# A four-layer graph network on one core: late transpositions of x, the last layer's scale and shift, and the order of the units behind the last score

## The chip, the cores and the metric

The kernel runs on one core of one Trainium2 chip. The metric is the device time of one execution in microseconds (us). The kernel before takes 3922.26 us, the median of three runs (3920.86 to 3927.18).

## What is computed

The input is x, 16 batches of 1024 nodes with 128 features, and one adjacency matrix of 1024 x 1024 that all batches share (about 1 in 64 entries set). Three attention layers follow each other, each with weights of its own, and then a fourth, last layer of another kind:

```python
# layers 0, 1, 2 (8 heads of 16)
Q, K, V = h @ Wq, h @ Wk, h @ Wv
scores = einsum('bnhd,bmhd->bhnm', Q, K) / 4
attn = softmax(where(adj == 0, -inf, scores))
x = layer_norm(h + (attn @ V) @ Wo + bo, ln1_g, ln1_b)
x = layer_norm(x + relu(x @ W1 + b1) @ W2 + b2, ln2_g, ln2_b)
# last layer
h = x @ W
e = leaky_relu((h @ a_src)[:, :, None] + (h @ a_dst)[:, None, :])   # slope 0.2
att = softmax(where(adj == 0, -inf, e))
out = ln_gamma * normalised(att @ h + x) + ln_beta
```

## The kernel before, in words

**Blocks and turns.** The work is cut into 48 blocks, each one attention layer of one batch. Four batches (LANES) form a group: layer 0 of the four, then layer 1 of the four, then layer 2 of the four, then the next group (L835). A block has 32 turns: two head groups g, two halves of the queries qh, eight tiles of keys kt. One turn of the main loop (L958 to L995) does a score step, an attention step four turns behind it (AHEAD), and one piece of the other work.

- The score step (L535) makes four matmuls of Q against K (L545), two for each of two PSUM slots "s". In most turns the first slot goes through ACT's exponential (L553) and is then multiplied by the mask on POOL (L554); the second gets the mask added on DVE (L557) and its exponential on ACT after that (L569). In the ten turns of BOTH_ON_DVE both go the second way, so POOL has no mask to do.
- The attention step (L574) multiplies the tile e by V and the row of ones, and accumulates in one bank. After eight steps, finish (L577) transposes the sums on DVE, takes reciprocals and multiplies on POOL (L589).

**Other work: chains of tasks.** Everything else stands in chains. A task is (gap, function, tiles, and for some a mark); put (L842) adds them, take (L852) runs one, is_due (L867) says when: `gap` turns after the task before it in the chain, or at the turn that a table AT gives for the chains "xP", "proj" and "post". piece (L871) runs once a turn: it takes every due task whose tiles text has a "*" (it uses no TensorE), but only one task without a star. That one task is called a unit below. "+w", "-x" and the like count work tiles taken and given back (TILES): x has five, one more than the lanes. need (L880) forces a chain on until a mark is done. All units share one PSUM bank "t"; edge units use the "s" slots.

**Who orders what.** PE, ACT and SP (the DMA queue that issues all loads and stores) run in the order in which the program is written, turn by turn. DVE and POOL are ordered by a scheduler, and issue_after pins some of their instructions behind the score step's.

**The x of the next group.** A batch's x is loaded (fetch, a unit of SP) when one of the five x tiles is free, that is, when a batch of the group before has stored its result. Where x is there by turn 22 two blocks ahead, its transposed copy is made through DRAM. Otherwise (late x) transpose_x (L496) with by_dma=False puts the two transpositions on TensorE (L345 in transpose_half) into the chain "xP", at turns 4 and 6 of the block ahead of its own. transpose_x also puts POOL's `scale` (multiplication by the gain of the layer before, L511, none for layer 0) and `shift` (addition of bo, L515), 6 or 2 turns on. Six projection units follow from turn 9 (AT_V_LAST), and stack (L523) lays Q and K out by DMAs on SP.

**The last layer** (last_tasks, L701) is a chain behind the last attention layer of each batch, so it runs in the blocks that follow it:

- xt(0), xt(1): two transpositions; nodes: three units of x @ W (L730 to L737) with POOL's multiplication of x by the gain (L798 in by_rows) taken behind the second and the addition of the bias behind the third;
- rows_gh (L742): one transposition of the per-node exponentials; send_rows (L749): eight DMAs on SP into the rows g_rows and h_rows (L756, L757);
- edges(v) (L761): eight matmuls from these rows (L769) and four DVE operations with the mask (L774) into an edge tile, of which there are two;
- aggregate(v) (L779): 32 matmuls (by_columns, L383), then DVE adds x (L785) and takes statistics. After v = 3 and v = 7, normalise scales four tiles on POOL (L433 to L435, L441);
- gain and bias of each half by POOL (by_rows, L798) and the stores on SP (L812), which give back the x tile.

Edge unit v+1 and aggregate v are one task, two turns from the one before.

**The end.** In the last block the halves of the queries are ordered so that the first half of its attention is complete earlier. Its post work runs as two short chains "final" (the list `alone`, L687: gather, output projection, x1t three turns later, two units of W1, one of W2), and the last layer of batch 15 behind them. After the last score turn (n = 1536) eight more main-loop turns take one unit each. Then the tail loop (L1002) counts turns on, and takes in each turn one due task of every chain.

Of the kernel before, what the change touches and what calls it, by code (L numbers as in the profile page):

```python
# [29 lines left out]
LANES = 4  # L30
FIRST = 1


AT = {"xP": (4, 6), "proj": (5, 7, 9, 11, 17, 19), "post": (13, 15, 17, 18, 21, 22, 22, 23, 24, 25, 27, 29, 31, 35, 38, 40)}
AT_V_LAST = (9, 11, 17, 19, 20, 21)
AT_FIRST = (12, 14, 16, 18, 20, 22)
T_AT = 22
STACK_AT = 24
AT_END = {3: (12, 21, 22, 24, 25, 26, 27, 28, 30, 31), 2: (8, 9, 13, 14, 15, 16, 17, 18, 20, 21)}
AHEAD = 4  # L40
BOTH_ON_DVE = (3, 7, 8, 15, 23, 24, 26, 28, 30, 31)
TILES = {"w": 8, "x": LANES + 1, "last": 2}
BLOCKED = -57344.0
# [76 lines left out]
def fast_path(ctx: ExitStack, tc: tile.TileContext, a: dict, out: bass.AP, flag):  # L120
# [375 lines left out]
    def transpose_x(m, by_dma=True):  # L496
        b, l = blocks[m]
        x, xT = state["x", b], xt_tile("xT")
        state["xT", m] = xT
        if by_dma:  # L500
            put(moved(lambda: xT, lambda: x), ("xT", m))
        elif m == 0:
            for h in range(2):
                transpose_half(xT[:, h], x, h)
        else:
            put([(0, lambda: transpose_half(xT[:, 0], x, 0), ""), (0, lambda: transpose_half(xT[:, 1], x, 1), "")],
                ("xP", m), first=True)

        def scale():
            with tc.issue_after(behind["pool"]) if m else nullcontext():  # L510
                nc.gpsimd.tensor_mul(x, x, rows(W[l - 1]["ln2_g"]))  # L511

        def shift():
            with tc.issue_after(behind["pool"]) if m else nullcontext():
                nc.gpsimd.tensor_add(x, x, rows(W[l]["bo"]))  # L515
        if m:
            put(([(6, scale, "*")] if l else []) + [(2 if l else 6, shift, "*")], ("shifted", m))
        else:
            shift()

# [73 lines left out]
    def post_tasks(m, quick=False):  # L594
        b, l = blocks[m]
        w = W[l]
        s = {}
        att, recs = state["A"], state["recs"]

        def gather(h):  # L600
            def run():
                s["aT", h] = half_tile("aT")
                nc.vector.transpose(s["aT", h], att[:, h].rearrange("p k g d -> p (k g d)"))
                if h == 1:
                    check_range(recs.rearrange("p g h k -> p (g h k)"))
            return run

        def out_proj(h):
            def run():
                if h == 0:  # L610
                    need_if(("shifted", m))
                    s["n1"] = with_stats(state["x", b])
                project([s["aT", h]], [w["Wo"]], h, add_and_stats(s["n1"]))
                normalise(s["n1"], slice(4 * h, 4 * h + 4))
            return run

        def x1t(h, alone=False):
            def run():
                x1 = s["n1"][0]
                if h == 0:  # L620
                    s["x1T"] = xt_tile("x1T")
                transpose_half(s["x1T"][:, h], x1, h)
                if alone:
                    scale_shift(x1[:, 4 * h:4 * h + 4, :], w["ln1_g"], w["b2"])
                elif h == 1:
                    scale_shift(x1, w["ln1_g"], w["b2"])
            return run

        def x1_by(op, v):
            def run():  # L630
                with tc.issue_after(behind["pool"]):
                    op(s["n1"][0], s["n1"][0], rows(w[v]))  # L632
            return run

        def normed(ts):
            def run():
                with tc.issue_after(behind["pool"]):
                    if ts.start == 0:
                        scalars(s["n2"], slice(0, NT))
                    subtract_scale(s["n2"], ts)  # L640
            return run

        def ffn1(f, h):
            def run():
                s["h", f, h] = half_tile("hT")
                ps = bank()
                by_columns(ps, w["W1"][:, f * P:(f + 1) * P], s["x1T"][:, h])
                with soon():
                    nc.scalar.activation(s["h", f, h], ps, AF.Relu, bias=w["b1"][:, f:f + 1], scale=1.0)  # L649
            return run  # L650

        def ffn2(h, alone=False):
            def run():
                if h == 0:
                    s["n2"] = with_stats(state["x", b])
                project([s["h", f, h] for f in range(NF)], [w["W2"][:, f, :] for f in range(NF)], h,
                        add_and_stats(s["n2"]))
                if alone:
                    normalise(s["n2"], slice(4 * h, 4 * h + 4))
            return run  # L660

        def both():
            with tc.issue_after(behind["dve"]):
                gather(0)()
                gather(1)()


        def x1():
            return s["n1"][0]

        def x1T():
            if "x1T" not in s:
                s["x1T"] = xt_tile("x1T")
            return s["x1T"]

        together = [(6, both, "+w +w *"), (1, out_proj(0), "-w"), (1, out_proj(1), "-w")]
        if quick:
            together += [(5, x1t(0), ""), (1, x1t(1), "")]
            together += [(1, ffn1(f, h), "+w") for h in range(2) for f in range(2)]
            together += [(1, ffn2(0, True), "-w -w"), (1, ffn2(1, True), "-w -w")]  # L680
        else:
            together += moved(x1T, x1)
            together += [(0, x1_by(nc.gpsimd.tensor_mul, "ln1_g"), "*"), (1, ffn1(0, 0), "+w"),
                         (0, x1_by(nc.gpsimd.tensor_add, "b2"), "*"), (1, ffn1(1, 0), "+w"), (2, ffn1(0, 1), "+w"),
                         (1, ffn1(1, 1), "+w"), (1, ffn2(0), "-w -w"), (1, ffn2(1), "-w -w"),
                         (3, normed(slice(0, 4)), "*"), (2, normed(slice(4, NT)), "*")]
        alone = [[(1, gather(h), "+w"), (1, out_proj(h), "-w"), (3, x1t(h, True), ""), (1, ffn1(0, h), "+w"),  # L687
                  (1, ffn1(1, h), "+w"), (1, ffn2(h, True), "-w -w")] for h in range(2)]
        return together, alone

# [10 lines left out]
    def last_tasks(b):  # L701
# [3 lines left out]
        def xt(h):  # L705
            def run():
                w = W[L - 1]
                if h == 0:

                    s["col"] = work.tile([P, 4, NT], F32, tag="col", name="col", bufs=2)  # L710
                    s["hd"] = [work.tile([P, 4, D + 1], F32, tag="w", name="hd", bufs=TILES["w"]) for _ in range(2)]
                    s["n"] = with_stats(state["x", b])
                s["xT", h] = half_tile("xT")
                transpose_half(s["xT", h], state["x", b], h, w["ln2_gc"], w["ln2_bc"])
            return run

        def nodes(t0, t1):
# [43 lines left out]
        def edges(v):  # L761
# [14 lines left out]
                                                   1.0, mask01[:, :, q:q + SLOT], op0=OP.max, op1=OP.mult)  # L776
            return run

        def aggregate(v):  # L779
            def run():  # L780
                e, ps = s["e", v], bank()
                for t in range(NT):
                    by_columns(ps[:, :D + 1], e[:, t, :], s["hd"][t // 4][:, t % 4, :], start=(t == 0), stop=(t == NT - 1))
# [1 line left out]
                nc.vector.scalar_tensor_tensor(s["n"][0][:, v, :], ps[:, :D], s["col"][:, 3, v:v + 1],  # L785
                                               state["x", b][:, v, :], op0=OP.mult, op1=OP.add)
                stats(s["n"], slice(v, v + 1))
                if v % 4 == 3:
                    with tc.issue_after(behind["pool"]):
                        normalise(s["n"], slice(v - 3, v + 1))  # L790
                if v == NT - 1:
                    check_range(s["col"].rearrange("p c t -> p (c t)"))
            return run
# [22 lines left out]
        def two(f, g):  # L816
            def run():
# [1 line left out]
                g()  # L819
            return run  # L820

        mul, add = nc.gpsimd.tensor_mul, nc.gpsimd.tensor_add
        tasks = [(5, xt(0), "+w +last +w +w"), (1, xt(1), "+w"), (2, nodes(0, 3), ""), (2, nodes(3, 6), ""),
                 (0, by_rows(mul, x, lambda: W[L - 1]["ln2_g"]), "*"), (2, nodes(6, 8), "-w -w"),
                 (0, by_rows(add, x, lambda: ln2_b_last), "*"), (2, rows_gh, ""), (1, send_rows, "*"), (7, edges(0), "")]
        for v in range(NT - 1):
            tasks.append((2, two(edges(v + 1), aggregate(v)), ""))
            if v in (4, 6):
                tasks.append((0, by_rows((mul, add)[v // 2 - 2], y(0), lambda v=v: wl[("ln_gamma", "ln_beta")[v // 2 - 2]], 4), "*"))
        tasks += [(2, aggregate(NT - 1), ""), (2, store(0), "-last -w -w *"), (1, by_rows(mul, y(1), lambda: wl["ln_gamma"], 4), "*"),  # L830
                  (2, by_rows(add, y(1), lambda: wl["ln_beta"], 4), "*"), (3, store(1), "-x *")]
        return tasks


# [17 lines left out]
    def take(chain):  # L852
# [3 lines left out]
            return False  # L856
        chain["queue"].popleft()
        f()
        for t in tiles.replace("*", "").split():
            free[t[1:]] += -1 if t[0] == "+" else 1  # L860
        done.add(mark)
        chain["due"] = now[0]
# [2 lines left out]
        return True  # L865

    def is_due(chain):  # L867
        gap, at = chain["queue"][0][0], chain["queue"][0][4]
        return now[0] >= max(chain["due"] + gap, at or 0)

    def piece():  # L871
# [371 lines left out]
```

## Time and profile before

| What | Value |
|---|---|
| runs, median (lowest to highest) | 3922.26 us (3920.86 to 3927.18) |
| the profiled execution, own time | 3922.55 us |
| its span | 3920.7 us |
| mean granted TensorE clock | 0.983 |
| PE busy | 3715.7 us |
| POOL busy | 3477.6 us |
| DVE busy | 3460.5 us |
| ACT busy | 3296.9 us |
| L554 (POOL's mask), one | 2029 ns, 1056 times |
| L574 (attention), one of the 12288 matmuls | 602 ns modelled, 1629.0 us busy in all |
| last score turn starts | 3800.1 us |

The trace gives every instruction its start, duration, and the idle time of its engine ahead of it in square brackets, with what ended it. "t" is the bank of the units, "acc" that of the attention step, "s" the slots of the scores. Times in the trace count from the start of the span, which is 1.85 us shorter than the execution's own time. Blocks and turns are not named in the trace; turn k of block m begins with the (32 m + k)th group of four L545 matmuls.

An ordinary block takes about 70.4 us. The blocks with last-layer work are longer: blocks 10 to 15 take 76.5, 94.2, 90.5, 92.4, 98.2 and 83.7 us, and those of the two groups after it are alike.

### The profile page before, as it was taken

Reading aid. Unit: us, or ns where it says so; the run is one execution under the profiler, and the core shown is the slowest. Engines: PE = TensorE matmul, PEld = TensorE weight load, DVE = VectorE, ACT = ScalarE, POOL = GpSimd, SP = SyncE. Lnnn points to the kernel's source line nnn. Section 1 sums busy time; section 2 is a strip of 40 time slices with the busy share of each in tenths; the row PEclk is TensorE's granted clock in tenths of the full one; section 3 lists DMA queues with packets and bytes.
Section 4 is the critical chain, followed back from the end, with each engine's and each line's share of the span. In section 5 each row is a group of like instructions: output and inputs, shape, how many; then the busy total and the mean of one; then the engine's idle time right before and its main releaser. Section 6 shows DMA issues by size and latency. Waiting matters only on the chain.

```text
span 3920.7 us, 109674 instructions
## 1 busy us (share of the span) xinstructions
PE 3715.7 (95%) x44385; PEld 1515.1 (39%) x44385; DVE 3460.5 (88%) x5860; ACT 3296.9 (84%) x3797; POOL 3477.6 (89%) x2971
## 2 busy tenths in 40 slices
PE   7999999999989999999998999999999999999987
PEld 2333333344434333334443333333444433333346
DVE  6999999989878999998897899998898889999876
ACT  7989999977877999997777899999777789999850
POOL 5899999988978999998878899999887899999885
PEclk8999999999999999999999999999999999999998
DMA  5424334322323334332222324334232323424200
GB/s 139 113 73 103 91 81 110 76 70 70 89 63 79 98 72 110 80 95 73 72 67 76 92 66 101 95 74 100 73 82 52 88 71 93 103 71 106 63 8 21
DMA packets 245887, 319.28 MB, mean 81 GB/s; under 512 B 51072, under 2 KB 174208, under 8 KB 245376
## 3 DMA queue, kind: packets, MB, share of 16 engines
q1 hardware_dynamic: 243840, 311.52, 31.7%
q8 instruction: 353, 5.78, 0.6%
q14 instruction: 158, 1.29, 0.1%
q10 hardware_dynamic: 1536, 0.68, 0.1%
HBM read 58.53 MB, written 51.38 MB: 28 GB/s over the span
## 4 chain that ended last, share of the span: by engine, by line
POOL 46%; PE 38%; ACT 5%; DVE 5%; issue 3%; SPq 2%; DMA 1%; DVEq 0%; ACTq 0%; POOLq 0%
POOL e L554 27%; PE acc L574 13%; PE t L383 12%; PE s L545 9%; POOL x L441 7%; POOL mv L435 4%; POOL x L632 4%; ACT e L553 3%; DVE e L557 3%; ACT e L569 2%; PE s L769 2%; POOL x L798 2%; PE s L383 1%; POOL A L589 1%; SPq L530 1%
## 5 line engine op out<-in xcount | busy, mean ns | idle before, releaser
L557 DVE TENSOR_TENSOR e<-s,mask_add 128x1024 f32<-128x1024 f32 x2016 | 2377.4, 1211 | 240.3 <-PE s L545 214.5
L554 POOL TENSOR_TENSOR e<-e,mask 128x1024 f32<-128x1024 f32 x1056 | 2120.1, 2029 | 241.6 <-ACT e L553 227.8
L569 ACT ACTIVATE e<-e 128x1024 f32<-128x1024 f32 x2016 | 2110.9, 1062 | 185.2 <-DVE e L557 156.3
L574 PE MATMUL acc<-e,v 128*17 128x512 f32 x12288 | 1629.0, 602 | 78.6 <-POOL e L554 64.8
L553 ACT ACTIVATE e<-s 128x1024 f32<-128x1024 f32 x1056 | 1083.3, 1026 | 250.6 <-PE s L545 244.8
L545 PE MATMUL s<-Wq,Wk 64*128 64x512 f32 x6144 | 1196.4, 458 | 32.3 <-DVE e L557 21.1
L545 PEld LDWEIGHTS s<-Wq,Wk 64*128 64x128 f32 x6144 | 499.8, 185 | 1085.2 <-issue 388.9
L574 PEld LDWEIGHTS acc<-e,v 128*17 128x17 f32 x12288 | 205.2, 96 | 595.2 <-issue 351.1
L441 POOL TENSOR_SCALAR x<-x,mv 128x128 f32<-128x128 f32 x896 | 388.1, 448 | 19.1
L435 POOL TENSOR_TENSOR mv<-mv,half_neg 128x4 f32<-128x4 f32 (+1 forms) x179 | 214.0, 1195 | 13.6
L413 DVE BATCH_NORM_STATS2 st<-x 128x6 f32<-128x128 f32 x896 | 204.0, 281 | 7.7
L383 PE MATMUL t<-hd,ee 128*32 128x129 f32 x6656 | 205.7, 275 | 2.5 <-DVE x L420 2.4
L383 PE MATMUL t<-x1T,W 128*32 128x512 f32 x1520 | 201.9, 603 | 0.3
L774 DVE SCALAR_TENSOR_TENSOR ee<-s,mask 128x256 f32<-128x256 f32 x512 | 179.8, 413 | 23.4 <-PE s L769 23.4
L383 PEld LDWEIGHTS t<-W,hT 128*32 128x32 f32 x6080 | 170.9, 111 | 59.5 <-issue 48.4
L383 PEld LDWEIGHTS t<-hd,ee 128*32 128x32 f32 x6656 | 178.8, 110 | 16.1 <-DVE x L420 5.8
L383 PE MATMUL t<-W,hT 128*32 128x128 f32 x6080 | 184.7, 274 | 0.1
L589 POOL TENSOR_TENSOR A<-tt,recs 128x256 f32<-128x256 f32 x192 | 119.8, 624 | 49.7 <-DVE recs L588 49.6
L420 DVE TENSOR_TENSOR x<-t,x 128x512 f32<-128x512 f32 x191 | 129.1, 676 | 38.3 <-PE t L383 38.0
L649 ACT ACTIVATE hT<-t,b 128x512 f32<-128x512 f32 x190 | 130.4, 686 | 23.3 <-PE t L383 22.5
L585 DVE STREAM_TRANSPOSE tt<-acc 128x512 f32<-128x512 f32 x192 | 135.3, 705 | 0.0
L357 DVE STREAM_TRANSPOSE xb<-x 128x512 f32<-128x512 f32 x164 | 115.0, 701 | 20.1 <-POOL x L441 19.9
(145 smaller groups left out, 2531.1 us busy)
## 6 DMA issues: line engine op xcount, KB each, us to landing
Wk<-hi SPq DMA_DIRECT2D x384, 128.0 KB
Wk<-lo SPq DMA_DIRECT2D x384, 128.0 KB
Wq<-hi SPq DMA_DIRECT2D x384, 128.0 KB
Wq<-lo SPq DMA_DIRECT2D x384, 128.0 KB
tr<-xb SPq DMA_DIRECT2D x656, 64.0 KB
x1T<-tr SPq DMA_DIRECT2D x90, 256.0 KB
xT<-tr SPq DMA_DIRECT2D x74, 256.0 KB
x<-in_x_dram SPq DMA_DIRECT2D x124, 64.0 KB
```

The source lines that it names most:

```text
L383: nc.tensor.matmul(dst[j:j + SLOT, :], cols, rhs, start=start, stop=stop)
L413: nc.vector.bn_stats(st[:, t, :], z[:, t, :])
L435: nc.gpsimd.tensor_tensor(v, v, half_neg[:, ts], OP.pow)
L441: nc.gpsimd.tensor_scalar(z[:, t, :], z[:, t, :], mv[:, t, 0:1], mv[:, t, 1:2], op0=OP.add, op1=OP.mult)
L545: nc.tensor.matmul(ps[:, r * 512:(r + 1) * 512], k[64 * r:64 * r + 64, kt * P:(kt + 1) * P], q[64 * r:64 * r + 64, q0:q0 + 512], start=Tru ...
L553: nc.scalar.activation(ev, psv, AF.Exp, scale=HD ** -0.5)
L554: behind["pool"] = nc.gpsimd.tensor_mul(ev, ev, m).ins
L557: behind["dve"] = nc.vector.tensor_add(ev, psv, m).ins
L569: nc.scalar.activation(ev, ev, AF.Exp, scale=HD ** -0.5)
L574: nc.tensor.matmul(acc[j * SLOT:j * SLOT + HD + 1, :], v_bufs[m % 2][:, kt, 2 * j + g, :], e[:, j, :], start=first, stop=last)
L589: nc.gpsimd.tensor_mul(state["A"][:, qh, :, g, :], tt[:, :, :HD], rec[:, :, None].to_broadcast([P, 16, HD]))
L774: nc.vector.scalar_tensor_tensor(e[:, :, j * SLOT:(j + 1) * SLOT], ps.rearrange("p (k q) -> p k q", q=P)[:, :, j * SLOT:(j + 1) * SLOT], 1 ...
```

## The change

It touches the planner alone; no operation is added, removed or resized.

- **Late x.** The two transpositions of a late x are due at turns 7 and 8 of the block, not 4 and 6. POOL's shift of a late x is due 31 turns after it is put, not 6.
- **Scale and shift of the last layer.** The multiplication and the addition of x leave the list of last-layer tasks. They become a chain of their own, "scaled", which xt(1) puts. A mark "~" in their tiles text lets them run only in turns 0 to 6, 22 and 23 of a block (POOL_FREE) as long as the tail has not begun. aggregate forces them if they have not run yet.
- **The fourth batch of a group** (not the very last batch): the normalisation of its second half is no longer part of aggregate(7) but a task after store(0). That task and the gain and bias of this half have the mark "^": turns 30, 31 and 0 to 6 only.
- **Behind the last score turn** (n of 1536 or more) a gap of 2 counts as 1, so a chain of last-layer units can take one unit every turn. The last batch's first edge unit follows its rows after 4 turns, not 7.
- **The end.** In the chain of the second half of the very last attention, x1t comes five turns after the output projection, not three.

```diff
-AT = {"xP": (4, 6), ...
+AT = {"xP": (7, 8), ...
+POOL_FREE = {"~": (0, 1, 2, 3, 4, 5, 6, 22, 23), "^": (30, 31, 0, 1, 2, 3, 4, 5, 6)}
...
-            put(([(6, scale, "*")] if l else []) + [(2 if l else 6, shift, "*")], ("shifted", m))
+            put(([(6, scale, "*")] if l else []) + [(2 if l else 6 if by_dma else 31, shift, "*")], ("shifted", m))
...
-        alone = [[(1, gather(h), "+w"), (1, out_proj(h), "-w"), (3, x1t(h, True), ""), ...
+        alone = [[(1, gather(h), "+w"), (1, out_proj(h), "-w"), (3 + 2 * h, x1t(h, True), ""), ...
...
                 transpose_half(s["xT", h], state["x", b], h, w["ln2_gc"], w["ln2_bc"])
+                if h == 1:
+                    put([(1, by_rows(mul, x, lambda: W[L - 1]["ln2_g"]), "*~"),
+                         (2, by_rows(add, x, lambda: ln2_b_last), "*~")], ("scaled", b), first=True)
...
+        late = b % LANES == LANES - 1 and b < B - 1
+
+        def norm(h):
+            def run():
+                with tc.issue_after(behind["pool"]):
+                    normalise(s["n"], slice(4 * h, 4 * h + 4))
+            return run
...
         def aggregate(v):
             def run():
+                need_if(("scaled", b))
...
-                if v % 4 == 3:
-                    with tc.issue_after(behind["pool"]):
-                        normalise(s["n"], slice(v - 3, v + 1))
+                if v % 4 == 3 and (v < NT - 1 or not late):
+                    norm(v // 4)()
...
-                 (0, by_rows(mul, x, lambda: W[L - 1]["ln2_g"]), "*"), (2, nodes(6, 8), "-w -w"),
-                 (0, by_rows(add, x, lambda: ln2_b_last), "*"), (2, rows_gh, ""), (1, send_rows, "*"), (7, edges(0), "")]
+                 (2, nodes(6, 8), "-w -w"), (2, rows_gh, ""), (1, send_rows, "*"), (7 if b < B - 1 else 4, edges(0), "")]
...
+        up = "*^" if late else "*"
+        tasks += [(2, aggregate(NT - 1), ""), (2, store(0), "-last -w -w *")] + [(0, norm(1), up)] * late
+        tasks += [(1, by_rows(mul, y(1), lambda: wl["ln_gamma"], 4), up), (2 - late, by_rows(add, y(1), lambda: wl["ln_beta"], 4), up),
+                  (3, store(1), "-x *")]
...
     def is_due(chain):
-        gap, at = chain["queue"][0][0], chain["queue"][0][4]
+        gap, tiles, at = chain["queue"][0][0], chain["queue"][0][2], chain["queue"][0][4]
+        if now[0] >= 4 * NT * len(blocks):
+            gap -= gap == 2
+        for c in POOL_FREE:
+            if c in tiles and not tail[0] and now[0] % (4 * NT) not in POOL_FREE[c]:
+                return False
         return now[0] >= max(chain["due"] + gap, at or 0)
```

More of the change, by code (lines that the diff above doesn't have):

```diff
@@ L31 @@
 FIRST = 1
-AT = {"xP": (4, 6), "proj": (5, 7, 9, 11, 17, 19), "post": (13, 15, 17, 18, 21, 22, 22, 23, 24, 25, 27, 29, 31, 35, 38, 40)}
+AT = {"xP": (7, 8), "proj": (5, 7, 9, 11, 17, 19), "post": (13, 15, 17, 18, 21, 22, 22, 23, 24, 25, 27, 29, 31, 35, 38, 40)}
 AT_V_LAST = (9, 11, 17, 19, 20, 21)
@@ L686, in post_tasks @@
                          (3, normed(slice(0, 4)), "*"), (2, normed(slice(4, NT)), "*")]
-        alone = [[(1, gather(h), "+w"), (1, out_proj(h), "-w"), (3, x1t(h, True), ""), (1, ffn1(0, h), "+w"),
+        alone = [[(1, gather(h), "+w"), (1, out_proj(h), "-w"), (3 + 2 * h, x1t(h, True), ""), (1, ffn1(0, h), "+w"),
                   (1, ffn1(1, h), "+w"), (1, ffn2(h, True), "-w -w")] for h in range(2)]
@@ L777, in edges @@
             return run
+        mul, add = nc.gpsimd.tensor_mul, nc.gpsimd.tensor_add
+        late = b % LANES == LANES - 1 and b < B - 1
[4 more added lines that the diff above has]
+            return run
         def aggregate(v):
             def run():
+                need_if(("scaled", b))
                 e, ps = s["e", v], bank()
@@ L820, in two @@
             return run
-        mul, add = nc.gpsimd.tensor_mul, nc.gpsimd.tensor_add
         tasks = [(5, xt(0), "+w +last +w +w"), (1, xt(1), "+w"), (2, nodes(0, 3), ""), (2, nodes(3, 6), ""),
-                 (0, by_rows(mul, x, lambda: W[L - 1]["ln2_g"]), "*"), (2, nodes(6, 8), "-w -w"),
-                 (0, by_rows(add, x, lambda: ln2_b_last), "*"), (2, rows_gh, ""), (1, send_rows, "*"), (7, edges(0), "")]
+                 (2, nodes(6, 8), "-w -w"), (2, rows_gh, ""), (1, send_rows, "*"), (7 if b < B - 1 else 4, edges(0), "")]
         for v in range(NT - 1):
@@ L829, in last_tasks @@
                 tasks.append((0, by_rows((mul, add)[v // 2 - 2], y(0), lambda v=v: wl[("ln_gamma", "ln_beta")[v // 2 - 2]], 4), "*"))
-        tasks += [(2, aggregate(NT - 1), ""), (2, store(0), "-last -w -w *"), (1, by_rows(mul, y(1), lambda: wl["ln_gamma"], 4), "*"),
-                  (2, by_rows(add, y(1), lambda: wl["ln_beta"], 4), "*"), (3, store(1), "-x *")]
+        up = "*^" if late else "*"
+        tasks += [(2, aggregate(NT - 1), ""), (2, store(0), "-last -w -w *")] + [(0, norm(1), up)] * late
+        tasks += [(1, by_rows(mul, y(1), lambda: wl["ln_gamma"], 4), up), (2 - late, by_rows(add, y(1), lambda: wl["ln_beta"], 4), up),
+                  (3, store(1), "-x *")]
         return tasks
@@ L858, in take @@
         f()
-        for t in tiles.replace("*", "").split():
+        for t in tiles.translate(str.maketrans("", "", "*~^")).split():
             free[t[1:]] += -1 if t[0] == "+" else 1
```

## The prediction

> **What bounds the kernel now.** I read the page first: TensorE (PE) is busy 95% of the span, so only the 5% it misses can be won.
>
> ```profile
> span 3920.7 us, 109674 instructions
> PE 3715.7 (95%) x44385; PEld 1515.1 (39%) x44385; DVE 3460.5 (88%) x5860; ACT 3296.9 (84%) x3797; POOL 3477.6 (89%) x2971
> PEclk8999999999999999999999999999999999999998
> ```
>
> Then the waits, longest first. Two of PE's own matter: for a DMA of x (three times, up to 7.8 us), and for POOL's masking of e (130 times).
>
> ```profile
> PE acc L574 <- POOL e L554: 64.8, 130, 2.5
> PE t L345 <- DMA x<-in_x_dram: 21.0, 3, 7.8
> ```
>
> Then the timelines of PE, SP and POOL around one such wait, in block 14 turn 4 (the four score matmuls of L545 mark a turn; blocks are counted from 0, 32 turns each). PE stands 7.80 us and starts again at half clock (1.22 us for a score step, otherwise 0.73).
>
> ```profile
> 1108.73 1.05 PE L574 MATMUL acc<-e,v 128*17 128x512 f32 x8
> 1117.58 1.08 PE L345 MATMUL t<-identf,x 128*128 128x128 f32 x4 [7.80 <-DMA x<-in_x_dram]
> 1118.59 1.22 PE L545 MATMUL s<-Wq,Wk 64*128 64x512 f32 x4
> ```
>
> ```profile
> 1090.31 20.66 SPq L812 DMA_DIRECT2D out_dram<-x  x8
> 1112.47 3.66 SPq L167 DMA_DIRECT2D x<-in_x_dram  x8
> ```
>
> ```profile
> 1099.87 2.02 POOL L554 TENSOR_TENSOR e<-e,mask 128x1024 f32<-128x1024 f32 x1 [9.59 <-ACT e L553]
> ...
> 1106.93 1.29 POOL L798 TENSOR_TENSOR x<-x,ln_beta 128x512 f32<-128x512 f32 x1
> ```
>
> The x to be loaded needs the tile of a batch whose last rows POOL finishes at 1108.2; SP's store waits for that, its load for the store, PE for the load (1117.6, 9.4 us after POOL).
>
> Last, the timeline after the final score step (3800.1):
>
> ```profile
> 3816.28 1.93 PE L383 MATMUL t<-Wo,aT 128*32 128x128 f32 x32 [5.07 <-DVE aT L603]
> ...
> 3822.50 1.76 PE L345 MATMUL s<-identf,x 128*128 128x128 f32 x4 [2.20 <-POOL x L441]
> ...
> 3857.55 1.08 PE L769 MATMUL s<-g_rows,h_rows 4*128 4x128 f32 x7 [5.21 <-DMA h_rows<-parts]
> ```
>
> **What the Trainium skill says.** "TensorE: Matmul & The Clock Gate", Part 1: after about 3.4 us of idleness PE runs at half clock until a busy window of that length. The trace agrees: granted clock 0.50 for 6.8, 10.2 and 6.8 us around the three x waits. Same page, Architectural detail: DVE, ACT and GpSimd queues are strictly in order; here a SyncE store likewise holds the loads behind it. "DMA: Bandwidth & Descriptors", Anatomy of one DMA: about 2 us fixed per transfer; here the last x issue ended at 1116.1 and PE was released 1.5 us later.
>
> **The change, part by part.** The sum is made against the profiled run (3922.55 us, of which the span is 3920.7); the median shown is 3922.26, so I take the saving off that. No operation is added or removed, so only waits count.
>
> *(1) Late x at turns 7 and 8 (blocks 14, 26, 38).* Turns 4 to 9 last 23.3, 23.4 and 22.7 us. A turn's PE work at full clock is 1.65 (0.66 scores, 0.98 L574), plus 0.59 for a transposition, 0.85 for a node unit, about 1.05 for the projection in turn 9. The same turns then need 2.50+1.65+2.50+2.25+2.25+3.2 (turn 9 as measured) = 14.35. Saved 9.0, 9.05, 8.35 = **26.4**. The x must be there by turn 7, some 8.7 us after the old place; it also comes sooner: the compiled order has the final normalisation of the batch that frees the tile before POOL's first mask of block 14, not after it, because its aggregation runs at turn 30, two turns earlier. That is some 6 us sooner, so the wait has cover twice. Moved past: the bo addition (2.40) goes to turn 31, where POOL idles 3.7 us before e of block 39 turn 0; free. Three consecutive units then hand over one PSUM bank: not shown in the trace, between 0 and 1 us a block in nine blocks; I take **-3** in all.
>
> *(2) POOL lighter in block 14.* bo (2.40) and scale and shift (2.39 each, before turns 9 and 11) leave the stretch where PE later waits 1.7 at turn 19 (DVE's xb behind POOL's L441) and 1.1 at turn 20. Both should go: 3 x 2.8 = **8.3**. The forced pair of units at the end of block 13 loses its gap of 0.8: **2.4**.
>
> *(3) Every fourth batch's last half-normalisation, gain and bias* (0.24+0.23+1.04+1.74+1.29+1.29 = 5.8 us of POOL) leave block 15 turns 6 to 11 for turn 30 to the next block's turn 0. Blocks 15, 27, 39 take 55.7, 56.3, 55.7 from turn 9 on; an ordinary block takes 51.3: **+13.8**. But the ordinary blocks that receive it are themselves bound by POOL: in block 40 the masks of turns 18 to 21 and 25 end 0.05 us before their L574. POOL idles there only 1.4+0.2 us before turn 6, so of 5.9 us about 4.1 comes back as PE waits (1.2 at turn 5, the rest near turn 18): 3 x -4.1 = **-12.3**.
>
> *(4) Scale at turn 22, shift at turn 0 (blocks 10/11, 22/23, 34/35, the first batch of four).* POOL's mask of turn 25 comes one 2.4 us operation earlier, and PE's 2.5 us wait in turn 29 shrinks. But the next block's first edge unit waits for rows in SP's queue, which is fixed by issue:
>
> ```profile
> 2731.59 0.72 SPq L756 DMA_DIRECT2D g_rows<-parts  x1
> ...
> 2741.72 0.60 SPq L757 DMA_DIRECT2D h_rows<-parts  x1
> ```
>
> They land at 2743.7, where PE already waits 0.66. Block 22 shows it: shorter by 1.5 than block 10, its next block stands 2.0 there. So **0** (bounds 0 and +12). For the second batch the order up to the mask that PE waits for is unchanged: 0. In the last block the multiplication leaves the queue ahead of turn 18's mask: its 2.44 us wait goes, and the half-clock window at 3773.4 with it (1.7): **4.1**.
>
> *(5) The tail.* From the last unit of batch 12 (3808.37) to that of batch 15 (3906.96) are 98.6 us. Its PE work at full clock, summed by unit (edges 0.59, aggregate 1.95, node units 2.25, transpositions 0.59 and so on) is 75.7. The rest is 13.6 of waits and 9.3 of half clock. With a unit every turn, batches 13 and 14, then 14 and 15, overlap. The 5.07 stays at 4.5 (the last attention's chain through POOL and DVE is the same; only one transposition fills it); 2.20 is covered by batch 13; the rows of batch 14 need 12.6 us from L742 to landing, and 11.4 us of units now lie between, so 5.21 becomes 1.2. I keep 4.5 of half clock and add 3 for two edge tiles shared by two batches at the change-over (each may wait one 1.39 us eviction, two or three times). Left 13.6 to 14, saved **9** (bounds 3 and 14). The chain after the last aggregate, 13.7 us of POOL and store, is unchanged.
>
> Sum: 26.4 - 3 + 8.3 + 2.4 + 13.8 - 12.3 + 0 + 4.1 + 9 = 48.7. **3922.3 - 48.7 = 3873.6, say 3874 us.**
>
> **Rivals.**
> *A, POOL takes more back.* The moved 5.8 us also delays the x1 normalisation in blocks 16, 28, 40, behind which DVE's xb stands (in block 39 a normalisation 6.5 us late cost 1.75 plus followers): -7 each; (2) and the last block give nothing, the tail 4. 26.4-3+13.8-21+4 = 20, so 3902. For it: the 0.05 us slacks. Against: POOL idles 24 us around block 14.
> *B, more is won.* Block 10's windows keep 12 and POOL's tax is only 6: 48.7+12+6 = 67, so 3855. Against it: the fixed landing of rows.
> *C, slower.* The shift now runs at turn 0, two turns before the first aggregate reads x. DVE is in order: if POOL came late, DVE would stand at L785 with the score additions behind it. The cost per place is POOL's lateness plus a half-clock window of 1.7; there are six such places, so it decides only from about 9.8 us each: 6 x 9.8 = 59, less the 48.7, some 10 slower: 3932. The trace speaks against it: POOL idles 3.1 to 3.4 us at that turn and would end the shift about 2.5 us ahead of L785.
> *D, nothing changes*, if x landed as late as PE reaches turn 7: against it, 8.7 us.
>
> **How the numbers follow.** Chances: main 0.66, A 0.14, B 0.13, C 0.04, D 0.03. The main case's own ends come from the tail (3 to 14) and POOL's tax (0 to -21), about 3863 to 3884. The range of 3854 to 3896 takes in B and most of the way to A. A difference of 0.2% (7.8 us) is about what a measurement can tell from none. Faster 0.92, same 0.03, slower 0.05.
>
> **What would show it.** Right: no PE wait for in_x_dram; turns 4 to 9 of block 14 near 14 to 15 us; block 15 near 79; block 16 near 74 where it was 70.7; block 11's first edge unit waiting 3 us or more for rows; last aggregate's end to span's end still near 13.7. Wrong: block 16 still at 70.5 (the tax was imagined), waits at L785 for POOL, or a tail still near 98 us between the two aggregates.

## The result, and the profile after

The changed kernel takes 3887.1 us (median of 4 runs, 3886.4 to 3887.5), the kernel before in the same comparison 3921.56: a ratio of 0.9909, 95% interval 0.9892 to 0.9926. That is 34.5 us less; 48.7 were forecast. The profiled executions differ by 35.8 us of span (3920.7 and 3884.9), and the account below is made between these two.

Where it went is read from the starts of the score turns: the start of turn 0 of a block to that of the next, summed over the three alike blocks of the three groups (us).

| Blocks | before | after | measured | forecast |
|---|---|---|---|---|
| 10, 22, 34 and 11, 23, 35 (first batch) | 228.0 + 288.7 | 217.9 + 303.2 | +4.4 | 0 |
| 12, 24, 36 | 271.6 | 284.6 | +13.0 | part of the +3 |
| 13, 25, 37 | 277.2 | 270.5 | -6.7 | -2.4 |
| 14, 26, 38 | 293.6 | 257.7 | -35.9 | -26.4 - 8.3 |
| 15, 27, 39 | 251.6 | 235.7 | -15.9 | -13.8 |
| 16, 28, 40 | 211.5 | 224.2 | +12.7 | +12.3 |
| block 47 to its last score turn | 103.0 | 100.3 | -2.7 | -4.1 |
| from there to the end | 120.6 | 115.4 | -5.2 | -9 |

All other blocks together are the same to 0.1 us; the start ahead of block 0 is 0.4 us longer. One line stands out: blocks 12, 24 and 36 cost 13 us that the forecast hardly had. The first row and the last two also differ by some us between kernels that are alike there; experiments 3 and 5 show by how much.

The page of the kernel after (its code lines are counted one higher than before from L42 on, and up to 18 higher towards the end):

```profile
span 3884.9 us, 109698 instructions
PE 3710.5 (96%) x44385; PEld 1513.9 (39%) x44385; DVE 3460.0 (89%) x5860; ACT 3295.4 (85%) x3797; POOL 3477.8 (90%) x2971
```

PE is busy 5.2 us less than before with the same 44385 matmuls: a matmul at half clock counts as busy for longer, so more could be won than the 5% in which PE is idle.

Its waits; the columns are engine and line, what it waited for, us in total, times, longest:

```profile
PE acc L575 <- POOL e L555: 57.0, 124, 2.5
PE s L773 <- DMA h_rows<-parts: 13.0, 5, 4.7
PE t L384 <- DVE lo L474: 10.0, 6, 2.2
```

The wait for in_x_dram (21.0 us before) is gone from the list. The wait for the rows has grown from 6.3 us in three to 13.0 in five. The third line looks like the one of before (9.7 us in 6, longest 1.7), but three of its six waits are new: 2.2 us each in turn 10 of blocks 12, 24 and 36, the other three of 1.1 us in turn 10 of blocks 14, 26 and 38.

PE and SP around the late transpositions of block 14. Turn 7 begins at 1119.31:

```profile
1119.31 0.73 PE L546 MATMUL s<-Wq,Wk 64*128 64x512 f32 x4
...
1120.95 0.66 PE L346 MATMUL t<-identf,x 128*128 128x128 f32 x4
```

```profile
1092.17 17.96 SPq L825 DMA_DIRECT2D out_dram<-x  x8
1111.63 4.60 SPq L168 DMA_DIRECT2D x<-in_x_dram  x8
```

No wait in brackets, full clock; turns 4 to 9 take 13.7 us (23.4 before, 14.35 forecast). The last load is issued by 1116.2; with the 1.5 us from issue to release of before it is there at 1117.7, 3.2 us ahead of the transposition at 1120.95. Counted from the block's start, POOL's last operation on the batch that frees the tile ends 5.2 us in, 10.1 before: 4.9 us sooner.

PE in the tail (the projection of the very last attention, the rows of the last batch, and the second of two aggregates that wait some 1.0 us for DVE):

```profile
3787.11 1.94 PE L384 MATMUL t<-Wo,aT 128*32 128x128 f32 x32 [4.48 <-DVE aT L604]
...
3844.21 1.20 PE L773 MATMUL s<-g_rows,h_rows 4*128 4x128 f32 x16 [0.80 <-DMA h_rows<-parts]
...
3852.70 3.76 PE L384 MATMUL s<-hd,ee 128*32 128x129 f32 x128 [1.03 <-DVE col L798]
```

The waits of 5.07, 2.20 and 5.21 us have become 4.48, none and 0.80, as forecast (4.5, none, 1.2).

### The profile page after: what moved, and what is told of

Same layout as the page of the kernel before. It is cut to its first block, busy times and chain, and to the rows that moved or that the text cites. A ratio compares the mean times of both kernels' runs of the same rounds, so it can differ in the third digit from the quotient of the medians.

```text
span 3884.9 us, 109698 instructions
## 1 busy us (share of the span) xinstructions
PE 3710.5 (96%) x44385; PEld 1513.9 (39%) x44385; DVE 3460.0 (89%) x5860; ACT 3295.4 (85%) x3797; POOL 3477.8 (90%) x2971
## 3 DMA queue, kind: packets, MB, share of 16 engines
q10 hardware_dynamic: 1536, 0.68, 0.1%
## 4 chain that ended last, share of the span: by engine, by line
POOL 45%; PE 38%; ACT 7%; DVE 5%; issue 3%; SPq 1%; DMA 1%; DVEq 0%; ACTq 0%; POOLq 0%
POOL e L555 27%; PE acc L575 13%; PE t L384 12%; PE s L546 9%; POOL x L442 6%; POOL x L633 4%; POOL mv L436 4%; ACT e L554 3%; ACT e L570 3%; DVE e L558 3%; PE s L773 2%; POOL x L811 1%; PE s L384 1%; POOL A L590 1%; POOL mv L435 1%
## 5 line engine op out<-in xcount | busy, mean ns | idle before, releaser
L555 POOL TENSOR_TENSOR e<-e,mask 128x1024 f32<-128x1024 f32 x1056 | 2120.1, 2029 | 215.3 <-ACT e L554 201.9
L384 PE MATMUL t<-hd,ee 128*32 128x129 f32 x6720 | 214.9, 280 | 7.0 <-DVE lo L474 6.6
L384 PEld LDWEIGHTS t<-hd,ee 128*32 128x32 f32 x6720 | 187.1, 112 | 22.6 <-issue 11.2
L384 PEld LDWEIGHTS t<-W,hT 128*32 128x32 f32 x6080 | 171.0, 111 | 59.3 <-issue 48.7
L650 ACT ACTIVATE hT<-t,b 128x512 f32<-128x512 f32 x190 | 130.8, 688 | 13.6 <-PE t L384 12.7
L358 DVE STREAM_TRANSPOSE xb<-x 128x512 f32<-128x512 f32 x164 | 115.1, 702 | 10.1 <-POOL x L442 9.8
```

The lines of the kernel that those rows point to most:

```text
L384: nc.tensor.matmul(dst[j:j + SLOT, :], cols, rhs, start=start, stop=stop)
L555: behind["pool"] = nc.gpsimd.tensor_mul(ev, ev, m).ins
```

## The experiments

The theory after the result: the parts add up, each in its own blocks; the missing 13 us are an order of DVE in blocks 12, 24, 36 that keeps the bank of the units; blocks 10 and 11 trade one wait for another; POOL alone sets the price in blocks 16. The rivals are named with each run. In the three comparisons that the kernels below stand in, the kernel before took 3923.65 (the first four), 3924.18 (the next four) and 3930.4 us (the last three); so block times are compared, and totals by their ratio to it.

**1. The late transpositions alone, and everything but them.**

```diff
 # late_x_only: the kernel before, with
-AT = {"xP": (4, 6), ...
+AT = {"xP": (7, 8), ...
-... [(2 if l else 6, shift, "*")], ("shifted", m))
+... [(2 if l else 6 if by_dma else 31, shift, "*")], ("shifted", m))
 # xp_4_6: the changed kernel, with
-AT = {"xP": (7, 8), ...
+AT = {"xP": (4, 6), ...
```

> The kernel before with the late transpositions at turns 7 and 8 and the late shift at 31 turns, nothing else. Theory (the parts stand alone): blocks 12 to 14 and their likes change as they did with the whole change, +13.0 -6.7 -35.7 = -29 us, blocks 10, 11, 15, 16 and the tail stay as before: about 3892 us, no wait of PE for in_x_dram. Rival (x comes in time only because the other parts empty POOL ahead of it): PE waits for x at turn 7 of blocks 14, 26, 38, some us each with a half-clock window behind it, 3900 to 3910.

> The changed kernel with the late transpositions back at turns 4 and 6. Theory: the wait for x is back in blocks 14, 26, 38 (about 7 us and a half-clock window each), blocks 12 lose their +4.3: 3887 + 29 = about 3916. Rival (most of the gain in block 14 is a lighter POOL, not the transpositions): 3900 or less, with block 14 below 92 us.

late_x_only: 3899.29 us, ratio 0.9939 (0.9923 to 0.9956). Blocks 12 to 14 and their likes take 284.8, 270.5 and 258.2: the change of 29 us is all here, the rest of the change adds nothing to it, and PE never waits for x. POOL's last operation on the batch that frees the tile ends 5.2 us into block 14 here too (10.1 in xp_4_6), so the earlier x comes of the place of the transpositions, not of a lighter POOL. The total is 7 us above the 3892 expected, most of it in the tail, which took 126.3 us in the profiled execution where the same tail took 120.6 before: one more stretch of half clock, 10.2 us long, behind a wait of 0.94 us.

xp_4_6: 3905.98 us, ratio 0.9955 (0.9938 to 0.9972). PE waits for x again, and at the end of block 13 for the gap of 0.81 us in the forced pair:

```profile
1100.39 1.98 PE L384 MATMUL t<-hd,ee 128*32 128x129 f32 x64 [0.81 <-DVE x L421]
...
1121.39 1.09 PE L346 MATMUL t<-identf,x 128*128 128x128 f32 x4 [7.45 <-DMA x<-in_x_dram]
```

Blocks 14, 26, 38 take 283.3: putting the transpositions back costs 25.6 us there, and the lighter POOL keeps the other 10.3. Both theories of this run got half. But the two causes overlap, as the turns of these three blocks show (us less than in the kernel before):

| Turns | changed | late_x_only | xp_4_6 |
|---|---|---|---|
| 4 to 9 | 28.8 | 28.8 | -0.1 |
| 10 | 1.2 | 1.2 | 0.0 |
| 19 and 20 | 5.2 | 4.9 | 9.5 |

Turns 4 to 10 belong to the transpositions alone. In turns 19 and 20 the lighter POOL gives 9.5 us while the transpositions stay, but 5.2 behind the moved ones. And late_x_only, with the scale and shift of the last layer in their old places, has nearly all of it: their leaving is worth 0.5 us in these blocks (257.7 against 258.2), and of POOL's load only the addition of bo, which has moved in all three, can have counted; no run moves the transpositions without it. Blocks 13, 25, 37 take 270.5 in late_x_only and 277.2 in xp_4_6, so their 6.7 us come of the place of the transpositions too, not of the lighter POOL.

**2. The order of DVE in blocks 12, 24, 36.** In the compiled order of the changed kernel, DVE's subtraction lo of a projection stands right behind an edge unit's four masks in three places, these blocks' turn 10; in the order of the kernel before in none. Each projection is followed by lo, and until lo has read the one bank of the units, no other unit can use it. PE and DVE of the changed kernel there:

```profile
941.34 1.07 PE L384 MATMUL t<-xT,Wk 128*32 128x512 f32 x8
...
943.98 0.66 PE L773 MATMUL s<-g_rows,h_rows 4*128 4x128 f32 x8
946.85 3.62 PE L384 MATMUL t<-hd,ee 128*32 128x129 f32 x64 [2.21 <-DVE lo L474]
```

```profile
943.34 1.21 DVE L558 TENSOR_TENSOR e<-s,mask_add 128x1024 f32<-128x1024 f32 x1
944.68 1.42 DVE L778 SCALAR_TENSOR_TENSOR ee<-s,mask 128x256 f32<-128x256 f32 x4
946.02 0.68 DVE L474 TENSOR_TENSOR lo<-t,hi 128x512 fp32r<-128x512 f32 x1
```

In the kernel before, at turn 10 of the same block, lo is done ahead of the masks, and the aggregate (on PE at 941.15) has no wait:

```profile
940.25 0.65 DVE L473 TENSOR_TENSOR lo<-t,hi 128x512 fp32r<-128x512 f32 x1
...
942.20 1.41 DVE L774 SCALAR_TENSOR_TENSOR ee<-s,mask 128x256 f32<-128x256 f32 x4
```

```profile
941.15 1.98 PE L383 MATMUL t<-hd,ee 128*32 128x129 f32 x64
```

In the changed kernel the aggregate waits 2.21 us and then takes 3.62 us (1.98 otherwise), at half clock. Two kernels take the order away in different ways: one by a pin, one by the turns.

```diff
 # lo_first, in edges(v)
+    with tc.issue_after(low[now[0] - 1]) if now[0] - 1 in low else nullcontext():
         nc.vector.scalar_tensor_tensor(e[:, :, j * SLOT:(j + 1) * SLOT], ...
 # xp_mixed, in transpose_x
-                ("xP", m), first=True)
+                ("xP", m), first=True, table=(4, 6) if b % LANES == 1 else None)
```

> The changed kernel; only the four DVE operations of an edge unit are pinned behind the DVE subtraction lo of the projection one turn earlier. Theory (in blocks 12, 24, 36 the scheduler put lo, which frees the bank of the units, behind the edge unit's masks, so PE waits 2.2 us at turn 10 and runs at half clock behind it): turn 10 falls from 8.0 to 4.1 us, 3 x 3.9 = 12 us less than the changed kernel, about 3875. Rival (the loss is that of three units in a row through one bank): no change, 3887.

> The changed kernel with the late transpositions at turns 4 and 6 for the second batch of a group only (blocks 12, 24, 36), 7 and 8 for the other two. Both theories: block 12 as before, 90.5 us, blocks 13 and 14 as changed: 3887 - 13 = about 3874. If the order of DVE were not the cause, the wait at turn 10 would stay: 3886.

lo_first: 3877.11 us, ratio 0.9881 (0.9865 to 0.9898); blocks 12, 24, 36 take 275.2. xp_mixed: 3876.39 us, ratio 0.9882 (0.9866 to 0.9899); 271.3, what they took before. DVE and PE with the pin:

```profile
945.20 1.22 DVE L558 TENSOR_TENSOR e<-s,mask_add 128x1024 f32<-128x1024 f32 x1
946.33 0.68 DVE L474 TENSOR_TENSOR lo<-t,hi 128x512 fp32r<-128x512 f32 x1
946.93 1.41 DVE L779 SCALAR_TENSOR_TENSOR ee<-s,mask 128x256 f32<-128x256 f32 x4
```

```profile
947.16 1.98 PE L384 MATMUL t<-hd,ee 128*32 128x129 f32 x64 [0.65 <-DVE lo L474]
```

lo and the masks have changed places, the wait has fallen from 2.21 to 0.65 us, and the aggregate runs at full clock. The order of these two was the cause of 9.4 of the 13.0 us. The 3.6 that remain with the pin and go with the old turns come of the place of the transpositions itself: 1.2 us a block, 0.65 of it the wait above.

**3. Scale and shift in their old places; the rows.**

```diff
 # scale_old: the chain "scaled" is not put; the tasks stand in the list again
-                 (2, nodes(6, 8), "-w -w"), (2, rows_gh, ""), ...
+                 (0, by_rows(mul, x, ...), "*"), (2, nodes(6, 8), "-w -w"),
+                 (0, by_rows(add, x, ...), "*"), (2, rows_gh, ""), ...
 # rows_later: lo_first, and for b % LANES == 0 the first two edge units in one task
+        if b % LANES == 0:
+            tasks.pop()
         for v in range(NT - 1):
+            if v == 0 and b % LANES == 0:
+                tasks.append((9, two(edges(0), two(edges(1), aggregate(0))), ""))
+                continue
```

> The changed kernel with POOL's scale and shift of the last layer back in its list of tasks. Theory (what POOL gives PE at turn 29 of blocks 10, 22, 34 is lost again at the rows, with a half-clock window more): these blocks get 10.1 us longer, blocks 11, 23, 35 14.5 shorter, block 47 2.7 longer: 2 us less than the changed kernel, about 3885. Rival (blocks 11, 23, 35 are longer because of the scaling order in themselves): they keep 101 us, and the kernel is 10 to 13 us slower, about 3899.

> The changed kernel with DVE's edge masks pinned behind lo, and for the first batch of each group the first edge unit taken in the turn of the second, two turns later; every later unit stays in its turn. Theory (what blocks 11, 23, 35 pay is the landing of the rows at a fixed time, 3.6 us of wait and a half-clock window): wait and window go but for about 1 us of DVE at the doubled unit, 3 us a place, 8 to 10 us less than with the pin alone (3877), about 3868. Rival (the time is only moved two turns on, since three units follow each other then): within 2 us of 3877.

scale_old: 3889.81 us, ratio 0.9913 (0.9896 to 0.993). Blocks 10, 22, 34 take 229.1 (217.9 changed), 11, 23, 35 take 291.9 (303.2), block 47 102.7 (100.3). So splitting off the scaling wins 11.2 us in the first blocks and pays 11.3 back in the next; block 47 gains 2.4 in this pair. The tail took 119.6 us, which is why the total is above the 3885 expected: PE waits for the rows there again,

```profile
3828.49 1.08 PE L770 MATMUL s<-g_rows,h_rows 4*128 4x128 f32 x7 [5.34 <-DMA h_rows<-parts]
```

where the longest wait for rows in the changed kernel's tail is 0.80. So the split serves the tail as well; why the rows are late without it, no run shows. One execution is not enough for blocks 10, 11 and their likes, though: the six executions with the split so far (the changed kernel, xp_4_6, lo_first, xp_mixed and, below, late_false and tail_old) give 521.1 to 524.8 us for both together, 523.2 in the mean; the three without (before, late_x_only, scale_old) 516.7 to 521.0, mean 518.4. The split costs about 5 us here in the mean of kernels that differ elsewhere, and most of it is half clock: these blocks have 23.9 to 30.7 us of it with the split and 17.1 to 27.3 without, and with half of that time taken off all nine stand at 507.4 to 509.8. PE and SP of the changed kernel at the border of the two blocks (817.70 is turn 0 of block 11):

```profile
819.36 0.32 PE L773 MATMUL s<-g_rows,h_rows 4*128 4x128 f32 x1
823.32 0.63 PE L773 MATMUL s<-g_rows,h_rows 4*128 4x128 f32 x7 [3.64 <-DMA h_rows<-parts]
...
824.94 1.91 PE L575 MATMUL acc<-e,v 128*17 128x512 f32 x8
```

```profile
811.42 0.79 SPq L760 DMA_DIRECT2D g_rows<-parts  x1
...
821.56 0.59 SPq L761 DMA_DIRECT2D h_rows<-parts  x1
```

Sixteen small transfers (eight into each of the two tiles of rows) leave SP one after the other in 10.7 us, the last at 822.15; PE, which came early, goes on 1.2 us later. In the kernel before PE came later, 0.9 us behind the end of the last of these issues (821.85), and had no wait:

```profile
822.77 0.89 PE L769 MATMUL s<-g_rows,h_rows 4*128 4x128 f32 x8
```

Behind the wait stands a half-clock stretch (an attention step of 1.05 us has become 1.91), which the forecast's zero left out: the three waits of PE only get back what turn 29 gave, the stretches come on top.

rows_later: 3869.46 us, ratio 0.9859 (0.9843 to 0.9875); blocks 11, 23, 35 take 293.1, 11.2 less than with the pin alone. PE there:

```profile
822.77 1.07 PE L773 MATMUL s<-g_rows,h_rows 4*128 4x128 f32 x15 [0.34 <-DMA h_rows<-parts]
823.92 2.95 PE L384 MATMUL t<-hd,ee 128*32 128x129 f32 x64
```

The rows were the cost, and it need not be paid: the wait is 0.34 us when two score turns are put ahead of it, and the half clock in these two rows falls from 27.3 us to 13.7. The total fell by less, since the edit also holds for batch 12 and the tail took 117.0 us (112.9 with the pin alone).

**4. POOL in blocks 15 and 16.**

```diff
 # late_false: the changed kernel, with
-        late = b % LANES == LANES - 1 and b < B - 1
+        late = False
 # pool_relief: rows_later, with
-            both = now[0] % (4 * NT) in BOTH_ON_DVE
+            both = now[0] % (4 * NT) in BOTH_ON_DVE + ((5, 19) if step[0] in (16, 28, 40) else ())
```

> The changed kernel without the move of the fourth batch's half normalisation, gain and bias. Theory (POOL has no idle time in an ordinary block, so what is moved there comes back nearly whole): blocks 15, 27, 39 get their 15.9 us back, blocks 16, 28, 40 lose their 12.7: 3 us slower than the changed kernel, about 3890. Rival (blocks 16 are longer for another reason): blocks 16 stay at 74.7 us, about 3903.

> rows_later with two masks of blocks 16, 28 and 40 (turns 5 and 19) on DVE in place of POOL: 2 x 2.03 us of POOL off, 2 x 1.21 us of DVE on, in each. Theory (POOL alone is full in these blocks): they fall from 74.7 to about 71 us, 10 us less in all. Rival (DVE and ACT are as full as POOL there): 74 us or more, within 3 us of rows_later or slower.

late_false: 3892.4 us, ratio 0.9918 (0.9902 to 0.9935). Blocks 15, 27, 39 take 251.7, blocks 16, 28, 40 211.6: what they took before, to 0.1 us. The move wins 16.0 and pays 12.6. POOL of the changed kernel at the start of block 16:

```profile
1273.39 1.30 POOL L811 TENSOR_TENSOR x<-x,ln_gamma 128x512 f32<-128x512 f32 x1
1274.65 2.03 POOL L555 TENSOR_TENSOR e<-e,mask 128x1024 f32<-128x1024 f32 x1
1276.63 1.29 POOL L811 TENSOR_TENSOR x<-x,ln_beta 128x512 f32<-128x512 f32 x1
1277.88 4.00 POOL L555 TENSOR_TENSOR e<-e,mask 128x1024 f32<-128x1024 f32 x2
```

No brackets: nothing lies idle between one and the next, and the mask at 1277.88 comes late, for which PE waits 1.36 us in turn 5.

pool_relief: 3864.25 us, ratio 0.9833 (0.9816 to 0.9849); blocks 16, 28, 40 take 215.3, 8.8 less than in rows_later. Two masks (4.06 us of POOL) moved to DVE give 2.9 us a block, so POOL is the bound there and DVE has room for two more.

**5. The tail.**

```diff
 # tail_old: the changed kernel, with
-        if now[0] >= 4 * NT * len(blocks):
-            gap -= gap == 2
-... (7 if b < B - 1 else 4, edges(0), "")
+... (7, edges(0), "")
-... (3 + 2 * h, x1t(h, True), "")
+... (3, x1t(h, True), "")
 # tail_fill: rows_later, with
-... (1, out_proj(h), "-w"), (3 + 2 * h, x1t(h, True), "")
+... (1 + 2 * h, out_proj(h), "-w"), (3, x1t(h, True), "")
 # rows_later_2 is rows_later once more
```

> The changed kernel with the old end: gaps of 2 behind the last score, 7 turns ahead of the last batch's first edge unit, 3 ahead of the last transposition. Theory (waits of 5.2, 2.2 and 5.2 us in place of 4.5, 0, 0.8 and two of 1.0; half-clock windows of 7 to 13 us either way): 5 to 9 us slower than the changed kernel, 3892 to 3896. Rival (the new end gains only by chance of the clock): within 2 us of it.

> The kernel of rows_later once more, as the base of the two others on the same chip: 3868 to 3871; its stretch behind the last score turn 112 to 118 us, by the length of the half-clock window.

> rows_later with the very last output projection three turns behind its transposition in place of one (and x1t in its old turn), so that batch 13's first two edge units and an aggregate stand ahead of it on PE. Theory (PE waits 4.5 us at that projection because nothing stands ahead of it, and the half-clock window of 7 to 13 us comes of this wait): 3.2 us of units fill it, the window goes: 6 to 10 us less than rows_later, about 3862. Rival (the chain from the last attention step through DVE and POOL sets the end anyway): within 2 us of rows_later.

tail_old: 3898.77 us, ratio 0.9933 (0.9917 to 0.995); from the last score turn to the end 122.9 us, 7.5 more than the changed kernel; the total is somewhat above the 3892 to 3896 expected. One pair does not give the price of the new end: the five executions that have it and no other change behind the last score turn (the changed kernel, xp_4_6, lo_first, xp_mixed, late_false) take 112.2 to 115.5 us there, 113.7 in the mean; the three with the old end (before, late_x_only, tail_old) 120.6 to 126.3, mean 123.3. The new end saves some 9.6 us in the mean. rows_later_2: 3871.64, ratio 0.9853 (0.9836 to 0.9869), with 114.9 behind the last score turn; rows_later had 117.0 with the same code. tail_fill: 3869.55, ratio 0.9847 (0.983 to 0.9863), 112.0 (3862 was expected). Its runs (3865 to 3872) overlap those of rows_later_2 (3866 to 3875), so whether it gains is not settled. What it did is seen on PE:

```profile
3764.76 1.12 PE L346 MATMUL t<-identf,x 128*128 128x128 f32 x4 [5.38 <-DVE x L421]
...
3773.57 3.82 PE L384 MATMUL t<-hd,ee 128*32 128x129 f32 x64 [2.91 <-DVE ee L779]
3778.13 1.08 PE L384 MATMUL t<-Wo,aT 128*32 128x128 f32 x32 [0.74 <-DVE x L800]
```

The edge matmuls fill part of the gap, but the aggregate behind them needs DVE's masks, and a wait of 2.91 us stands there in place of the 4.48 at the projection. The half-clock window did not go, and the theory had its origin wrong: it opens at 3762.8, within the wait of 5.38 us ahead of a transposition, which rows_later has as well (at 3764.51) and the changed kernel has not. It lasts 13.7 us here and 23.9 in rows_later.

## Why the prediction was right, and where it was wrong

The direction, the place of the gain and the range held; the sum was 14 us too good. Its steps:

- *(1) Late x.* Right in mechanism and size: turns 4 to 9 became 28.8 us shorter against 26.4, and late_x_only has the same 28.8. "The wait has cover twice" was too much, though: x came 4.9 us sooner, not 6, and 3.2 us are left. By these numbers PE would have waited 1.7 us at turn 7 without the earlier arrival (4.9 less 3.2), so both covers were needed; this is an estimate, and no run tried it.
- *"Three consecutive units then hand over one PSUM bank ... I take -3 in all."* This is the step that failed. The place itself costs 1.2 us in each of blocks 12, 24, 36 (3.6 in all). But the moved transpositions shift the edge units by a turn, and with this the scheduler put DVE's lo behind their masks: 3.1 us more in each, 9.4 in all. The turns of the units were worked out ahead, the order that DVE got from them was not read.
- *(2) POOL lighter in block 14.* 5.2 us in turns 19 and 20 against 8.3: "Both should go" was half right, the 1.7 us at turn 19 went and the 1.1 at turn 20 stayed. Scale and shift had almost no part in it (4.9 without their move). In blocks 13 the 0.8 us gap went as said, but the 2.4 stood under the wrong cause: the gap is gone in late_x_only and back in xp_4_6, so it is the place of the transpositions, and the blocks gained 6.7. That blocks 14 match the forecast (35.9 and 34.7) is in part luck: too little under (1) against too much under (2).
- *(3) The fourth batch.* Right: 15.9 won (13.8), 12.7 paid (12.3), and by what it said, POOL without idle time in the block that receives the work.
- *(4)* "So 0" had the wait for the rows right, but no half-clock stretch behind it, although the x waits of before show one each: it is +4.4 in the table, about +5 over all executions. Block 47: 2.7 against 4.1, since its turn 30 took 1.3 longer (scale_old has this too, so it is not the split). The executions with the split took 100.1 to 102.2 us there, those without 102.7 to 104.0.
- *(5) The tail.* The waits fell from 13.6 to 7.8 us, near the forecast. The "4.5 of half clock" was too little for this execution: a window of 13.6 us stood behind the 4.48 us wait, 6.8 us lost. By the measure of the forecast, from the last unit of batch 12 to the end of the last aggregate, 98.6 us became 91.7: 6.9 saved, not 9. Over the executions of experiment 5 the saving is 9.6 in the mean, so 9 was a good figure, and how near one pair comes to it is the luck of the half-clock windows. The chain behind the last aggregate took 13.9 us, 13.7 forecast.

*Rivals.* A's main item (blocks 16 at +7 each) did not come (+4.2). B's low tax did not either, nor D: PE waits for no x. C's mechanism, DVE standing behind POOL at the addition of x, is in no list of waits; but its kind, something queued ahead of what PE needs on the in-order DVE, is what cost the most, with lo and the masks in place of x.

## What to carry to other kernels

Where a scheduler orders an engine, moving units by a turn can reorder what stands behind them: compare the compiled order of every engine, and look for an operation that frees a shared buffer and now stands behind one that could wait. Work moved off one stretch of a saturated engine is worth the idle time that it finds in the next; here 12.7 of 15.9 us came back. And a wait that ends with a transfer from a busy queue takes back whatever arrives earlier, until other work is put ahead of it: rows_later with two masks moved to DVE (pool_relief) is the fastest version here, 0.9833 of the kernel before (which was some 6 us slower in that comparison than in the others).

## What the runs showed of the hardware

Stretches at half clock last whole multiples of 3.4 us in these traces (3.4, 6.8, 10.2, 13.7 and 23.9 us behind waits), but for the one that the end of the program cuts off. The granted clock of the changed kernel behind the 4.48 us wait, and that of xp_mixed behind the same wait (start and end; the share of full clock is the number after the POOL column):

```profile
3784.00:3789.00 5.00, 1.89 (x34) 1.54 (x34) 0.71 (x1) 0.00 (x0) 4.76 (x9) 0.78 0.00 0
3789.00:3794.00 5.00, 4.60 (x57) 3.96 (x58) 4.47 (x17) 0.00 (x0) 4.24 (x8) 0.50 0.20 52
3794.00:3799.00 5.00, 5.00 (x82) 4.28 (x78) 2.37 (x8) 0.00 (x0) 0.57 (x2) 0.50 0.01 3
3799.00:3804.00 5.00, 5.00 (x128) 4.31 (x124) 2.63 (x10) 0.78 (x1) 2.66 (x2) 0.86 0.01 3
```

```profile
3775.00:3780.00 5.00, 1.32 (x28) 1.35 (x32) 0.77 (x2) 0.01 (x1) 4.70 (x11) 0.87 0.00 0
3780.00:3785.00 5.00, 4.62 (x57) 3.60 (x53) 4.31 (x17) 0.00 (x0) 4.25 (x7) 0.50 0.20 52
3785.00:3790.00 5.00, 5.00 (x125) 4.36 (x119) 3.17 (x12) 0.17 (x1) 1.31 (x4) 0.94 0.01 3
```

Twice the missing share of each slice gives the length: 5 x 2 x (0.22 + 0.50 + 0.50 + 0.14) = 13.6 us in one, 5 x 2 x (0.13 + 0.50 + 0.06) = 6.9 in the other, with the same units and the same wait. A wait of 2.5 us at turn 29 of block 11 opened a stretch of 3.4 us in the changed kernel and none in the kernel before. This fits what the Trainium skill says in "TensorE: Matmul & The Clock Gate", Part 1, of a free-running window of 3413 ns: where a wait falls in it would then decide; no run here moves one wait through the window. The two lengths above, 13.6 and 6.9 us at half clock, differ by 3.4 us of time, so by this estimate the price of a wait is uncertain by some 2 us each way. Behind the last score turn the same code took 114.9 and 117.0 us. A total alone can't tell a tail edit of 2 us; the lists of waits can.
